# Start-up order of a fused window-attention and Fourier-mixing kernel: bias of image 1, load of the next image, norm of image 2, quarters and eighths

## The chip, the core and the metric

The kernel runs on one core of a Trainium2 chip. A core has a matrix engine (TensorE: PE, with its weight loads as PEld), a vector engine (VectorE: DVE), an activation engine (ScalarE: ACT), GpSimd (POOL), and SyncE (SP), which here only issues DMAs. The metric is the device time of one execution in microseconds (us).

## What is computed

The input `x` has 32 images of 56 x 56 pixels with 128 channels, in fp32. Two layers follow each other, each with a residual. `_gn` is a group norm over an image: 32 groups of 4 channels.

```python
x = x + _L0_conv_ref(_gn(x), ...)   # shifted-window attention
x = x + _L1_conv_ref(_gn(x), ...)   # Fourier mixing, then a feed-forward layer

# layer 0: roll by 3, windows of 7 x 7, 4 heads of 32 channels
qkv  = win @ w_qkv.T
attn = softmax(q @ k.T * scale + rel_bias + mask)
out  = (attn @ v) @ w_proj.T + b_proj              # then roll back

# layer 1: along the width with w0, along the height with w1
y = idct(einsum('bixy,ioy->boxy', dct(x)[..., :32], w))
b = relu((y0 + y1) @ W1 + b1) @ W2 + b2
```

## The kernel before

**The unit of work.** A window row is 7 lines of an image, 8 windows, 392 tokens. An image has 8 window rows. The outer loop counts `cycle`; cycle `r` begins window row `r % 8` of image `r // 8` and carries on older rows and images. A cycle does:

- `attn_qk` for row r: two matmuls on PE, q (L380) and half of k (L389) written by ACT, the other half of k (L397) by DVE. They need `im.w`, the image's scaled weights (`wn`, L364), and `im.bias`.
- `attn_scores` for row r (called in `quarters`): PE L431, then two DVE additions of bias and mask (L439) out of two PSUM banks.
- `attn_max`: a DVE maximum (L449) and a POOL subtraction (L450); `attn_exp` on ACT (L456); `attn_divide`: DVE sum (L461), reciprocal (L463), POOL product (L464).
- `attn_transpose` of earlier rows: PE L475, copies by DVE (L485) and ACT (L483).
- `attn_values` for row r-3 (called in `eighths`): PE L500 into two banks; bank 0 is copied to `oT` by ACT (L533), bank 1 by three DVE instructions (L531).
- `attn_v` for row r (PE L409, copied by ACT L416) and `attn_project` for row r-3: PE with `wproj`, a DVE addition into the image (L548) and a DMA to the scratch tensor `scr`.
- `attn_sums` for row r-4: statistics for layer 1 (DVE L562, ACT L570, DVE L571).

**The Fourier stages.** From cycle 11 on, `fourier(cycle)` names the images in layer 1 and their step c: width transforms at c = 0, height transforms at 1 and 2 (of columns loaded from `scr` into `htok` by `load_columns`), `mix` at 3 to 5 (PE L680, copied by ACT L688), `modes_back` at 5 to 8 (PE L719; ACT L735 or DVE L730 out of PSUM) and feed-forward groups at c in 8, 9, 10, 12 to 15. A cycle is "without feed-forward" if no image in it is at such a c. That holds for every cycle before 19 and, until the last image, for one cycle in eight afterwards.

**PSUM.** There are eight banks, four for attention (`pa`) and four for layer 1 (`pc`). A matmul waits until the last reader of its bank is through.

**Begin of an image.** `image_begin(b)` takes one of two buffers `xl` and loads half of the image; the other half is loaded in the next cycle. `image_groups` transposes it on PE into `xw`, takes statistics, and adds the projection's bias to the image on POOL by `image_bias` (L307, two instructions for two window rows). For image 0 `image_bias` is called in cycles 0 to 3 instead. `image_groups` runs in cycles 4 and 5 for image 1, and in cycle 6 of every eight for the later ones.

**Norm of an image.** `image_norm` is a generator that is driven in four steps, one per `next(norm, None)`: (1) nothing; (2) a chain of twelve small DVE instructions (L334 to L352) and a power on POOL (`rstd`, L356); (3) `nb` on DVE (L361) and `wn` on ACT (L364); (4) a bias by four matmuls and a copy (L368).

**Order.** PE, ACT, DVE and POOL run in exactly the order in which the program calls them: the loop is inside `tc.manual_schedule(engines={ET.PE, ET.Activation, ET.DVE, ET.Pool})`. SP is not in this set. The order of its DMAs is made when the program is built, from the written order and from a model of when their buffers and data are ready.

The calls of a cycle are `first_rows` for cycles 0 to 10. After that they are `halves_first`, (`half_columns`), `eighths`, `quarters`, `full`, `halves_last`. `next_begin` at the end of a cycle starts the load of the next image:

```python
if b + 1 < NB and i == 3:
    images[b + 1] = image_begin(b + 1)
if b + 1 < NB and i == 4 and images[b + 1].half:
    load_part(images[b + 1].x, b + 1, 1)
```

Of the kernel before, what the change touches and what calls it, by code (L numbers as in the profile page):

```python
# [24 lines left out]
NWR = S // WS  # L25
# [23 lines left out]
def swin_fourier_kernel(  # L49
# [20 lines left out]
    nc = tc.nc  # L70
    NB = x.shape[0]
# [195 lines left out]
    def image_groups(im, i):  # L267

        pt = [conv_bank() if i % 4 else attn_bank() for _ in range(2)]
        pts = [
            p[:, : n * S].rearrange("p (j r s) -> p j r s", r=n, s=WS) for p, n in zip(pt, (8, 6))
        ]
        for c in range(7):
            nc.tensor.transpose(  # L276
                pts[c // 4][:, :, 2 * (c % 4) : 2 * (c % 4) + 2],
                im.x[:, WS * i // 2 + c],
                ident_x[:, :, SS:].rearrange("p r (j s) -> p j r s", s=WS),
            )  # L280
        for k in range(2):

            im.xw[i + k] = big.tile([P, RT + JP - WT], F32, tag="xw", name="xw", bufs=10)
            nc.gpsimd.memset(im.xw[i + k][:, RT:], 0.0)
            xw = im.xw[i + k][:, :RT]
            dst = xw.rearrange("p (j r s) -> p j r s", r=WS, s=WS)
            if k:
                nc.scalar.copy(dst[:, :, 0], pts[0][:, :, WS])
                nc.scalar.copy(
                    dst[:, :, 1:].rearrange("p j r s -> p j (r s)"),  # L290
                    pts[1].rearrange("p j r s -> p j (r s)"),
                )
            else:
                nc.scalar.copy(
                    dst.rearrange("p j r s -> p j (r s)"),
                    pts[0][:, :, :WS].rearrange("p j r s -> p j (r s)"),
                )
            nc.vector.bn_stats(im.st[:, i + k], xw)
        if im.b:
            image_bias(im, i)  # L300

    def image_bias(im, i):
# [182 lines left out]
                nc.vector.tensor_copy(aT[:PW, :, :PW], src)  # L485
            im.aT[i].append(aT)

    def attn_values(im, i, r):


        v = v_sb[r % 3]
        po = [attn_bank(), attn_bank()]
        HALF = RT // 2
        po4 = [p[:, :HALF].rearrange("p (r n s) -> p n r s", r=WS, s=WS) for p in po]
        for f in range(2):
            for e in range(2):
                for h in range(NH):
                    for u in range(2):
                        ks = slice(u * JP, u * JP + WT)
                        nc.tensor.matmul(  # L500
                            po4[u][h * HD : (h + 1) * HD, 2 * f + e],
                            lhsT=v[ks, 2 * f + e, h * HD : (h + 1) * HD],
                            rhs=im.aT[i][f][ks, h, e * JP : e * JP + WT],
                            start=True,
                            stop=True,
                        )

        if i % 2 == 0:
            im.oT = work.tile([P, 2 * RT], F32, tag="oT", name="oT")
        oT = im.oT  # L510


        oTr = oT[:, i % 2 * RT : (i % 2 + 1) * RT].rearrange("p (r x) -> p r x", x=S)
        for u in range(2):
            src = po[u][:, :HALF].rearrange("p (r f x) -> p r f x", r=WS, f=2)
            x0 = SS + u * 2 * WS
            if not u:
                dst = bass.AP(
                    oTr.tensor, oTr[:, :, x0:].offset, [oTr.ap[0], [S, WS], [4 * WS, 2], [1, 2 * WS]]
                )  # L520
                parts = [(dst, src)]
            else:
                n = S - 4 * WS - x0
                parts = [
                    (oTr[:, :, x0 : x0 + 2 * WS], src[:, :, 0]),
                    (oTr[:, :, S - n : S], src[:, :, 1, :n]),
                    (oTr[:, :, 0:SS], src[:, :, 1, n:]),
                ]
            for d, f in parts:
                if u:  # L530
                    nc.vector.tensor_scalar(d, f, im.bias[:, 2:3], None, ALU.add)  # L531
                else:
                    nc.scalar.activation(d, f, AF.Identity, bias=im.bias[:, 2:3])  # L533
# [322 lines left out]
    def halves_first(cycle, norm):  # L856
        for im, c in fourier(cycle):
            if c == 0 and cycle > CONV_BEGIN:
                start_stats(im)
        last, j = row(cycle - 4)  # L860
        sums = attn_sums(last, j) if last and cycle > CONV_BEGIN else nothing()
        next(sums)
        im, i = row(cycle)
        if im:
            attn_qk(im, i, False)
        if has_ff(cycle):
            next(norm, None)
        next(sums)
        for im, c in fourier(cycle):
            if c in FF_AT:  # L870
                ff_in(im, FF_AT.index(c))
        for im, c in fourier(cycle):
            if c == 0:
                next(im.stats)
# [38 lines left out]
    def eighths(cycle):  # L913
        im, i = row(cycle - 3)
        if im:
            attn_values(im, i, cycle - 3)

    def full(cycle):

# [19 lines left out]
    def halves_last(cycle, norm):  # L939
        im, i = row(cycle)  # L940
        if im:
            attn_v(im, i, cycle)
        if has_ff(cycle):
            half_columns(cycle)
        half_columns(cycle, True)
        load_back(cycle + 1)
        next_begin(cycle)
        load_first(cycle)
        next(norm, None)
        if row(cycle)[0]:  # L950
            attn_exp(cycle)
            attn_divide(cycle)
        im, j = row(cycle - 3)
        if im:
            last_out(cycle)
            attn_project(im, j)

    def next_begin(cycle):
        b, i = divmod(cycle, NWR)
        if b + 1 < NB and i == 3:  # L960
            images[b + 1] = image_begin(b + 1)
        if b + 1 < NB and i == 4 and images[b + 1].half:
            load_part(images[b + 1].x, b + 1, 1)


# [1 line left out]
    def first_rows(cycle, norm):  # L967
        im, i = row(cycle)
        if im:
            attn_qk(im, i, True)  # L970
        if cycle:
            attn_exp(cycle - 1)
        im3, i3 = row(cycle - 3)
        if im3:
            attn_values(im3, i3, cycle - 3)
        im2, i2 = row(cycle - 2)
        if im2:
            attn_transpose(im2, i2, cycle - 2)
        if cycle:
            attn_divide(cycle - 1)  # L980
        if im:
            attn_scores(im, i, cycle)
            attn_max(cycle)
        if im3:
            attn_project(im3, i3)
        next(norm, None)
        last, j = row(cycle - 4)
        if last:
            for _ in attn_sums(last, j):
                pass  # L990
        if im:
            attn_v(im, i, cycle)
        if cycle < NWR // 2:
            image_bias(im, 2 * cycle)
        if cycle in (4, 5):
            for half in range(2):
                bias_and_mask(nc.gpsimd, 1, cycle - 4, half)
        next_begin(cycle)
        next_groups(cycle)
        if cycle == CONV_BEGIN - 1:  # L1000
            start_stats(im3)
            for _ in attn_sums(im3, i3):
                pass
            attn_exp(cycle)
            attn_divide(cycle)
            last, j = row(cycle - 1)
            attn_transpose(last, j, cycle - 1)

    ET = mybir.EngineType
    with tc.manual_schedule(engines={ET.PE, ET.Activation, ET.DVE, ET.Pool}):  # L1010
# [6 lines left out]
        for cycle in range(NB * NWR + CONV_BEGIN + FF_AT[-1] - NWR + 1):  # L1017
            if cycle < CONV_BEGIN:
                first_rows(cycle, norm)
            else:  # L1020
                halves_first(cycle, norm)
                if not row(cycle - 3)[0]:
                    half_columns(cycle)
                    half_columns(cycle, True)
                    load_first(cycle)
                    last_out(cycle)
                    quarters(cycle)
                    load_back(cycle + 1)
                    continue
                if not has_ff(cycle):  # L1030
                    half_columns(cycle)
                eighths(cycle)
                quarters(cycle)
                if not has_ff(cycle):
                    next(norm, None)
                if row(cycle)[0] and cycle % 2:
                    attn_max(cycle)
                full(cycle)
                halves_last(cycle, norm)
            b, i = divmod(cycle, NWR)  # L1040
            if i == (NWR - 2 if b else NWR - 3) and b + 1 < NB:
                norm = image_norm(images[b + 1])
                next(norm, None)
# [62 lines left out]
```

## Time and profile before

| what | value |
|---|---|
| median of 3 runs | 3616.99 us (3616.63 to 3623.41) |
| profiled execution | 3612.19 us, span 3610.4 us |
| PE busy | 3553.3 us, 98% of the span |
| PEld, DVE, ACT, POOL busy | 78%, 63%, 59%, 38% |
| DMA | 390.30 MB, 16 engines busy 39% to 40% |
| granted TensorE clock, mean | 0.997 |

The profile shows one execution. "Busy" is the time in which an engine works on an instruction; a wait names the engine and line whose instruction ended last before the waiting one began. "L450" is line 450 of the kernel. The window view gives the busy time of each engine within a stretch, and the clock that TensorE was granted there (1.00 is full speed). The timeline lists instructions of one engine in order of time, neighbours of one kind merged. Cycle 4 begins at about 45 us, cycle 7 at 67 us, cycle 8 at 82 us, cycle 12 at 114 us, cycle 15 at 149 us, cycle 16 at 159 us, cycle 17 at 171 us, cycle 18 at 178 us and cycle 19 at 191 us, counted by the first q matmul.

### The profile page before, as it was taken

To read this page: it belongs to the slowest core of one execution; us is meant where nothing else is said; L and a number is where in the kernel's file an instruction comes from. 1 tells how busy PE (TensorE), PEld (TensorE's weight loads), DVE (VectorE), ACT (ScalarE), POOL (GpSimd) and SP (SyncE) were. 2 spreads that over 40 slices of the span, in tenths; PEclk is the share of its full clock that TensorE was granted. 3 is DMA by queue.
4 is the path that set the end of the run, shared out by engine and by line. 5 is a ranking of instruction groups with operands and counts; after the bars stand their busy time and mean duration, and the time that the engine had idled before them with its cause. 6 is when DMAs were issued, how large, how long until landed. Compare 5 with 4: busy or idle time off the path is not lost.

```text
span 3610.4 us, 161666 instructions
## 1 busy us (share of the span) xinstructions
PE 3553.3 (98%) x72192; PEld 2827.3 (78%) x72192; DVE 2256.6 (63%) x4722; ACT 2145.8 (59%) x4044; POOL 1375.3 (38%) x1437
## 2 busy tenths in 40 slices
PE   7899999999999999999999999999999999999999
PEld 5778787777877787877777777878777877777776
DVE  7766666665666666666656666666666666666641
ACT  5555566665666655666556666556665566655553
POOL 6443343433443433434333434343443344343411
PEclk9999999999999999999999999999999999999999
DMA  4334433444434444344444344443444443444343
GB/s 115 95 101 110 118 104 103 109 111 111 111 98 115 109 109 120 98 109 107 114 106 115 95 111 112 112 117 93 112 108 115 107 114 95 114 109 114 95 117 97
DMA packets 687349, 390.30 MB, mean 108 GB/s; under 512 B 39967, under 2 KB 657600, under 8 KB 686400
## 3 DMA queue, kind: packets, MB, share of 16 engines
q1 hardware_dynamic: 686045, 379.65, 39.0%
q8 instruction: 568, 9.31, 1.1%
q14 instruction: 125, 1.02, 0.1%
q10 hardware_dynamic: 611, 0.32, 0.0%
HBM read 218.29 MB, written 161.48 MB: 105 GB/s over the span
## 4 chain that ended last, share of the span: by engine, by line
PE 93%; DVE 4%; ACT 1%; issue 1%; POOL 1%; DMA 0%; SPq 0%; ACTq 0%; POOLq 0%; DVEq 0%
PE pc L112 38%; PE pa L112 15%; PE pa L409 6%; PE pc L680 6%; PE pa L475 6%; PE pc L646 6%; PE pa L431 5%; PE pa L500 4%; PE pc L719 4%; PE pa L276 1%; PE pc L276 1%; DVE a L439 1%; DVE xf L730 0%; DVE oT L531 0%; POOL rstd L617 0%
## 5 line engine op out<-in xcount | busy, mean ns | idle before, releaser
L450 POOL TENSOR_TENSOR a<-a,mx 128x784 f32<-128x784 f32 x256 | 389.8, 1523 | 1390.3 <-DVE mx L449 954.1
L112 PE MATMUL pc<-wff,hid 128*64 128x128 f32 x12544 | 739.9, 273 | 1.5 <-ACT hid L764 1.0
L112 PE MATMUL pc<-xf,wff 128*64 128x512 f32 (+2 forms) x3584 | 718.2, 539 | 1.1 <-DVE xf L730 1.0
L112 PEld LDWEIGHTS pc<-wff,hid 128*64 128x64 f32 x12544 | 702.5, 137 | 7.7 <-ACT hid L764 4.6
L461 DVE TENSOR_REDUCE sm<-a 128x16 f32<-128x784 f32 x256 | 248.3, 970 | 674.2 <-ACT a L456 670.9
L464 POOL TENSOR_TENSOR a<-a,rs 128x784 f32<-128x784 f32 x256 | 389.7, 1522 | 609.1 <-DVE rs L463 553.8
L764 ACT ACTIVATE hid<-pc,b1sb 128x512 f32<-128x512 f32 (+2 forms) x896 | 522.4, 631 | 71.9 <-PE pc L112 68.5
L112 PEld LDWEIGHTS pc<-xf,wff 128*64 128x64 f32 x3584 | 275.7, 137 | 358.9 <-issue 240.3
L380 ACT ACTIVATE q<-pa,bqkv 128x392 f32<-128x392 f32 x256 | 150.5, 588 | 463.1 <-PE pa L112 457.4
L112 PE MATMUL pa<-xw,wn 128*64 128x392 f32 (+1 forms) x2048 | 389.0, 495 | 9.0 <-ACT wn L364 8.3
L531 DVE TENSOR_SCALAR oT<-pa,bqkv 128x98 f32<-128x98 f32 (+2 forms) x768 | 171.1, 278 | 242.5 <-PE pa L500 242.4
L456 ACT ACTIVATE a<-a 128x784 f32<-128x784 f32 x256 | 222.7, 870 | 150.8 <-POOL a L450 148.8
L752 POOL TENSOR_TENSOR res<-res,b2sb 128x512 f32<-128x512 f32 (+2 forms) x256 | 264.6, 1039 | 113.8 <-DMA res<-scr 107.5
L416 ACT COPY v<-pa 128x512 f32<-128x512 f32 x256 | 151.1, 590 | 243.3 <-PE pa L409 243.2
L307 POOL TENSOR_TENSOR xl<-xl,bproj 112x512 f32<-112x512 f32 (+1 forms) x256 | 287.5, 1146 | 0.1
L409 PE MATMUL pa<-wn,xw 128*64 128x128 f32 x4096 | 283.5, 280 | 3.5 <-issue 1.7
L500 PEld LDWEIGHTS pa<-aT,v 49*32 49x32 f32 x16384 | 172.3, 105 | 145.6 <-issue 119.5
L439 DVE TENSOR_TENSOR a<-pa,bm 128x392 f32<-128x392 f32 x512 | 264.9, 560 | 26.5 <-PE pa L431 2.7
L483 ACT COPY aT<-pa 113x452 f32<-113x452 f32 x256 | 139.7, 546 | 208.6 <-PE pa L475 205.3
L475 PE MATMUL pa<-ident,a 113*113 113x113 f32 x2048 | 242.9, 271 | 7.1 <-POOL a L464 3.8
L409 PEld LDWEIGHTS pa<-wn,xw 128*64 128x64 f32 x4096 | 221.3, 137 | 36.0 <-issue 3.2
L449 DVE TENSOR_REDUCE mx<-a 128x16 f32<-128x784 f32 x256 | 246.4, 962 | 4.3
(97 smaller groups left out, 5647.7 us busy)
## 6 DMA issues: line engine op xcount, KB each, us to landing
zscr<-z SPq DMA_DIRECT2D x512, 112.0 KB
htok<-scr SPq DMA_DIRECT2D x256, 196.0 KB
zT<-zscr SPq DMA_DIRECT2D x192, 256.0 KB
res<-scr SPq DMA_DIRECT2D x160, 256.0 KB
out_dram<-res SPq DMA_DIRECT2D x160, 256.0 KB
scr<-xl SPq DMA_DIRECT2D x128, 224.0 KB
xl<-in_x_dram SPq DMA_DIRECT2D x32, 784.0 KB
xl<-in_x_dram SPq DMA_DIRECT2D x32, 672.0 KB
```

What stands on the lines that cost most here:

```text
L112: nc.tensor.matmul(dst[ps], lhsT=lhsT[:, ps], rhs=rhs, start=start, stop=stop)
L307: nc.gpsimd.tensor_tensor(piece, piece, bproj.unsqueeze(1).to_broadcast([TC, e - a, C]), ALU.add)
L409: nc.tensor.matmul(pv[hs, j * C : (j + 1) * C], lhsT=im.xw[i][:, w * WT : w * WT + JP], rhs=im.w[:, 2 * C : 3 * C], start=True, stop=True,)
L439: nc.vector.tensor_tensor(a[:, 2 * hp : 2 * hp + 2, :, 0:WT].rearrange("p u w j -> p w u j"), ps[hp][:, :RT].rearrange("p (w u j) -> p w u ...
L449: nc.vector.tensor_reduce(mx, a3, axis=AX.X, op=ALU.max)
L450: nc.gpsimd.tensor_tensor(a3, a3, mx.unsqueeze(2).to_broadcast([P, 2 * NWR, WT]), ALU.subtract)
L461: nc.vector.tensor_reduce(sm, a3, axis=AX.X, op=ALU.add)
L464: nc.gpsimd.tensor_tensor(a3, a3, rs.unsqueeze(2).to_broadcast([P, 2 * NWR, WT]), ALU.mult)
L475: nc.tensor.transpose(pt[:PW, h * P : h * P + PW], a[:PW, h, 2 * hf : 2 * hf + 2].rearrange("p w j -> p (w j)")[:, :PW], ident[:PW, :PW],)
L500: nc.tensor.matmul(po4[u][h * HD : (h + 1) * HD, 2 * f + e], lhsT=v[ks, 2 * f + e, h * HD : (h + 1) * HD], rhs=im.aT[i][f][ks, h, e * JP : ...
L752: nc.gpsimd.tensor_tensor(res[:m, c0:c1], res[:m, c0:c1], b2sb[:m].unsqueeze(1).to_broadcast([m, c1 - c0, C]), ALU.add,)
L764: nc.scalar.activation(hf[:, :n], ph[:, :n], AF.Relu, bias=b1sb[:, f : f + 1])
```

## The change

1. `image_bias` for image 1 moves out of `image_groups` (cycles 4 and 5) into `first_rows`, one call in each of the cycles 6 to 9.
2. `next_begin` starts the next image at i = 4 instead of 3 and loads its second half at i = 5 instead of 4. `load_first` is called ahead of it.
3. In cycles without feed-forward the step of the norm that stood after `quarters` now stands in `halves_first`, ahead of the scores. This touches steps 2 and 4 of image 2's norm, in cycles 15 and 16. In cycle 15 the three DVE copies of `attn_values` (L531) become ACT instructions.
4. In cycles without feed-forward that have back groups, `quarters` is called ahead of `eighths`. These are cycles 16, 17 and 18.

```diff
-        if im.b:
+        if im.b > 1:
             image_bias(im, i)
...
-    def attn_values(im, i, r):
+    def attn_values(im, i, r, copies):
...
-                if u:
+                if copies[u] is nc.vector:
                     nc.vector.tensor_scalar(d, f, im.bias[:, 2:3], None, ALU.add)
...
-        if has_ff(cycle):
-            next(norm, None)
+        next(norm, None)
         next(sums)
...
-            attn_values(im, i, cycle - 3)
+
+            copies = (nc.scalar, nc.vector)
+            if cycle % NWR == NWR - 1 and not has_ff(cycle):
+                copies = (nc.scalar, nc.scalar)
+            attn_values(im, i, cycle - 3, copies)
...
         load_back(cycle + 1)
+        load_first(cycle)
         next_begin(cycle)
-        load_first(cycle)
         next(norm, None)
...
-        if b + 1 < NB and i == 3:
+        if b + 1 < NB and i == 4:
             images[b + 1] = image_begin(b + 1)
-        if b + 1 < NB and i == 4 and images[b + 1].half:
+        if b + 1 < NB and i == 5 and images[b + 1].half:
             load_part(images[b + 1].x, b + 1, 1)
...
         if cycle < NWR // 2:
             image_bias(im, 2 * cycle)
+        elif cycle >= NWR - 2 and cycle < NWR + 2:
+            image_bias(images[1], 2 * (cycle - NWR + 2))
...
-                eighths(cycle)
-                quarters(cycle)
-                if not has_ff(cycle):
-                    next(norm, None)
+                if has_ff(cycle) or not any(back_groups(c) for _, c in fourier(cycle)):
+                    eighths(cycle)
+                    quarters(cycle)
+                else:
+                    quarters(cycle)
+                    eighths(cycle)
```

## The prediction

> **What bounds the kernel now.** I read the page's busy table first (PE busy 3553.3 us, 98% of the span), then the stages by windows. In this view the columns are: window, its length, busy time of PE, PEld, DVE, ACT, POOL (instructions), granted clock, DMA share, GB/s.
>
> ```profile
> 68.30:71.60 3.30, 1.22 (x68) 0.67 (x64) 3.20 (x5) 1.77 (x3) 3.30 (x6) 1.00 0.46 124
> 71.70:81.80 10.10, 6.95 (x68) 6.18 (x70) 9.69 (x21) 2.74 (x5) 5.55 (x5) 0.50 0.00 0
> 160.50:163.70 3.20, 3.20 (x34) 3.20 (x30) 2.43 (x5) 2.98 (x8) 1.10 (x1) 0.50 0.00 0
> 264.00:3358.00 3094.00, 3083.68 (x63168) 2463.74 (x63166) 1972.58 (x4116) 1870.82 (x3529) 1193.47 (x1232) 1.00 0.40 109
> ```
>
> From 264 us to 3358 us PE lacks 10 us in 3094: nothing of weight can be won there, only lost. The idle time is in the first 200 us, and there the granted clock falls to 0.50 after some gaps. So the next view is PE's waits in that stretch (total us, times, longest):
>
> ```profile
> PE pa L112 <- ACT wn L364: 8.3, 2, 5.1
> PE pa L475 <- POOL a L464: 3.8, 2, 3.4
> PE pa L431 <- ACT k L393: 3.1, 2, 1.7
> PE pa L500 <- issue: 2.2, 1, 2.2
> PE pa L475 <- DVE a L439: 1.8, 1, 1.8
> ```
>
> Two of these the change touches: 3.41 us in cycle 7 (transposes wait for POOL) and 3.26 us at the start of cycle 16 (first matmul of image 2 waits for its scaled weights, wn). The timeline shows what precedes the first, POOL's and DVE's own queues (start, duration, engine, line):
>
> ```profile
> 69.17 2.23 POOL L307 TENSOR_TENSOR xl<-xl,bproj 112x512 f32<-112x512 f32 x2
> 71.34 1.53 POOL L464 TENSOR_TENSOR a<-a,rs 128x784 f32<-128x784 f32 x1
> 72.82 1.52 POOL L450 TENSOR_TENSOR a<-a,mx 128x784 f32<-128x784 f32 x1
> ```
> ```profile
> 69.44 3.47 DVE L325 TENSOR_SCALAR gmeans<-gsums 128x32 f32<-128x32 f32 x1
> 72.94 1.45 DVE L340 TENSOR_TENSOR turned<-turned,gmeans 128x32 f32<-128x32 f32 x1
> 74.42 0.19 DVE L341 TENSOR_TENSOR turned<-turned 128x32 f32<-128x32 f32 x1
> 76.50 0.66 DVE L531 TENSOR_SCALAR oT<-pa,bqkv 128x98 f32<-128x98 f32 x3
> ```
>
> L464's input was ready at 66.1 (reciprocal L463, 65.84 + 0.25); it starts 5.2 us later, behind image 1's bias (L307). Two tiny DVE steps of the norm, 0.18 and 0.19 us elsewhere, last 3.47 and 1.45 us while POOL works, and hold L531, for which PE's scores wait. One pair of steady rows shows the same in every later image, where the norm runs beside POOL:
>
> ```profile
> 807.15 0.56 DVE L325 TENSOR_SCALAR gmeans<-gsums 128x32 f32<-128x32 f32 x1
> 807.75 1.45 DVE L340 TENSOR_TENSOR turned<-turned,gmeans 128x32 f32<-128x32 f32 x1
> 810.31 0.15 DVE L352 SCALAR_TENSOR_TENSOR ve<-back 128x1 f32<-128x1 f32 x1
> ```
>
> **Bias of image 1 (cycles 4, 5 to 6-9).** POOL loses four calls of 2.24 us, 9.0 us, ahead of L464 of row 5. L464 then runs at 66.2-67.7 and L450 of row 6 (mx ready 68.06) at 68.2-69.7. On DVE, L325 is let in at about 69.75 in place of 72.91, L340 takes 0.19, the rest of the chain 1.26 (75.66 - 74.39), so it ends near 71.3 in place of 75.66; two reductions (0.55 each) and L531 follow, to 73.0. PE transposes at 69.6 and can do the last 28 scores at 73.1 where it did them at 77.3: 4.2 us. In that cycle the scores, projection and v took 1.57 + 1.47 + 1.67 = 4.7 us at clock 0.50; the same steps two cycles earlier took 0.89 + 0.80 + 0.87 = 2.6. PE's idle time there falls from 5.3 us to about 1.75, so I take the clock as full: 2.1 more. Against it: nb (L361) still waits for POOL's L450 (1.29 us before, likewise after) and DVE, nearly full in cycle 8, is late for its copies: 0.6 back. Term: -5.7; ends -6.3 and -3.0 (clock halved again and DVE later). The moved bias, 2.24 us in each of cycles 6 to 9, lies in POOL's idle time, which is 2.8, 4.7, 3.6 and 2.9 us ahead of the next L464; without that cover each call would cost up to 2.24.
>
> [...]
>
> **Norm of image 2 ahead of scores (cycles 15, 16), its copies on ACT.** In cycle 15 the chain starts at 153.1 in place of 155.18. But POOL is busy to 155.84 with L307 and L464, as in the steady rows above, where the chain takes 4.2 us (806.29 to 810.46) in place of 2.5 (155.18 to 157.72). So ve comes 0.45 us earlier, and wn with it: the 3.26 us gap shrinks to 2.8. The chain now stands ahead of L571, the scores' two L439 (1.03) and the maximum L449, which ends 1.2 us later; behind L449 are POOL's L450, ACT's exp, the q and k copies and z copies of cycle 16. The three oT copies go to ACT, which idles 1.36 us before L416: nothing. In cycle 16 PE's four bias matmuls only change place.
>
> [...]
>
> **Quarters ahead of eighths (cycles 16, 17, 18; no others lack feed-forward and have back groups).** The second back group needs the banks of the two z copies. They end at 164.64; now near 165.8. Scores (0.8), values (0.75), transposes (1.78) follow: cycle 16's v starts at 169.9 in place of 169.28, +0.6. In cycle 17 the values (0.74) used to run while PE waited for k (L397); now they come after the scores, and L531 (0.66) stands between L439 and L449. Scores wait for L397 till 176.3 (175.39 before), and cycle 18 starts at 179.6 in place of 177.85. In cycle 18 DVE's L730 (2.2) no longer follows L531, which gives 0.35 back: +1.4 at cycle 19. PE's gaps of 1.7 to 2.9 us in these cycles may halve the clock as at 160.5; I add 0.6 (a 3.4 us window loses at most 1.7, mostly behind other waits). Term of cycles 15 to 18: +2.0; ends -3.3 (the gap of cycle 16 goes and nothing comes back) and +4.5.
>
> **Image load a cycle later.** SP's order is not the written one:
>
> ```profile
> 59.37 0.38 SPq L745 DMA_DIRECT2D res<-scr  x1
> 109.73 4.55 SPq L118 DMA_DIRECT2D xl<-in_x_dram  x5
> ```
>
> A load of cycle 19 (190 us) is issued at 59 us, and both halves of image 2 go together though written a cycle apart: SP takes what has its buffer. The buffer is free once the width transforms of cycle 3 of the 8 have read it, before and after alike. So I expect the same issue times: 0. The htok loads are ahead of it already (860.4 against 867.5 in one image), and the reordering of `load_first` does nothing. If the load does move, image 2's leaves cycle 12, where PE's 2.19 us "issue" gap fell in the same stretch as that load and cost 2.6 us more at half clock: -4.8. It is needed in cycle 6 of the 8, some 14 us after SP would then issue it, so a move alone starves no one.
>
> **Sum.** -5.7 + 2.0 + 0 = -3.7 us. The profiled execution was 3612.19 us (span 3610.4, 1.8 around it), 4.8 below the median of 3616.99; the difference goes onto the median: 3613.3. Less than 0.2% (7.2 us) is about what a measurement of this kernel cannot tell from no change.
>
> **Rivals.** *More than expected (0.22).* The load leaves cycle 12 (-4.8), with the other terms as above: 3608.5. For it: the gap lies where the load's traffic saturated the DMA. Against it: SP's issue order just shown.
> *The gain does not arrive (0.14).* DVE and the half clock hold cycle 7 to -3.0 and cycles 15 to 18 give +3 back: 3617. For it: DVE is busy 9.69 of 10.10 us in the window of cycle 7. Against it: most of that is blocked time.
> *Slower (0.11).* The load does move a cycle and meets PE's instruction stream in a dense stretch of every image, as it may have in cycle 12: 2.19 us in each of 30 images is +66, 3679; a fifth of the images gives 3626. It decides from 0.36 us an image ((7.2 + 3.7)/30). Against it: in the new place, the end of the next cycle, the same kinds of step follow.
>
> **How the numbers follow.** The forecast, within 0.2%, has 0.53: its own range is 3609 to 3618. Faster by over 0.2%: 0.20 of the first rival and 0.04 of the forecast's tail, 0.24. Slower: 0.09 of the last and 0.01 of the second, 0.10. The rest, 0.66, is the same. The range 3606.5 to 3620 leaves out about 0.08 below and 0.11 above.
>
> **What would show it.** Right: L464 of row 5 starts by 66.5 us, L325 in cycle 6 under 1 us, cycle 8 starts 5 to 6 us earlier; the wait for wn in cycle 16 is still over 2 us; L325/L340 in cycle 15 last 0.5 and 1.4 us; xl is still issued right after the width transforms; later images take 110.1 us as now (first q matmul to first q matmul, eight cycles on). Wrong: xl a cycle later, no "issue" gap in cycle 12, a wait for wn under 1 us, or other than 110.1 us an image.

## The result and the profile after

The changed kernel took 3617.97 us (median of 4 runs, 3614.64 to 3620.66) and the kernel before 3619.18 us (4 runs, 3616.63 to 3623.41): a ratio of 0.9995, interval 0.9978 to 1.0012, no difference that this measurement can tell. (The prediction's 3616.99 us is the median of the first three of these four runs; the fourth took 3621.37.) In a longer comparison (e13_after_again below) the ratio was 0.9991, interval 0.9982 to 1.0000. The forecast had been 3613.3 us in a range of 3606.5 to 3620.

The windows of after's profile that answer to those of before come first: cycle 7, then the gap of cycle 16, then the later images (columns as before: window, length, busy PE, PEld, DVE, ACT, POOL, granted clock, DMA share, GB/s).

```profile
71.20:74.60 3.40, 2.36 (x77) 1.74 (x76) 3.02 (x14) 3.11 (x7) 1.79 (x3) 1.00 0.29 71
74.60:81.40 6.80, 6.14 (x62) 5.07 (x64) 6.66 (x13) 1.43 (x4) 5.85 (x5) 0.51 0.10 26
...
153.10:156.50 3.40, 1.08 (x8) 0.48 (x8) 3.19 (x9) 0.61 (x1) 0.55 (x1) 1.00 0.63 189
156.60:160.00 3.40, 3.40 (x36) 3.18 (x34) 0.87 (x3) 1.64 (x5) 1.52 (x1) 0.50 0.02 5
...
264.00:3358.00 3094.00, 3080.59 (x63062) 2459.66 (x63060) 1969.27 (x4106) 1868.73 (x3524) 1189.01 (x1229) 1.00 0.41 109
```

In the first of these windows PE idles 1.04 us of 3.40 (its gaps in cycle 7 add up to 1.6 us, before to 5.3), and still the clock is halved for the 6.8 us that follow. After 264 us PE lacks 13 us in 3094 where it lacked 10.

PE's waits in the first 200 us of after (total us, times, longest):

```profile
PE pa L112 <- ACT wn L364: 7.8, 2, 5.1
PE pa L431 <- DVE k L397: 5.8, 3, 2.4
...
PE pa L500 <- issue: 1.6, 1, 1.6
...
PE pa L475 <- POOL a L464: 0.4, 1, 0.4
```

The wait for POOL's L464 has gone from 3.8 to 0.4 us. The wait for k (L397) is now 5.8 us in three places; before it was 2.3, 1.70 in cycle 14 and 0.58 in cycle 17. Now 1.69 of it is in cycle 17 and 2.43 in cycle 18. These two come with the quarters; what they cost is taken up with the prediction's term below.

The stages, each from the first q matmul of one cycle to that of another, in us, worked out from the profiled execution of each kernel. "Half" is the time between 60 and 200 us in which the granted clock was 0.50.

| kernel | 4-8 | 8-12 | 12-15 | 15-20 | 24-248 | half |
|---|---|---|---|---|---|---|
| before | 37.1 | 32.3 | 35.0 | 59.8 | 3094.3 | 20.5 |
| after | 32.9 | 33.2 | 33.2 | 62.4 | 3100.6 | 20.5 |
| e13_after_again | 32.7 | 33.2 | 33.5 | 62.4 | 3095.4 | 20.5 |
| e1_bias | 32.0 | 32.7 | 36.6 | 60.1 | 3096.8 | 20.5 |
| e12_bias_again | 30.5 | 33.7 | 34.1 | 59.7 | 3097.8 | 6.8 |
| e2_load | 37.0 | 32.7 | 34.7 | 60.2 | 3096.3 | 17.1 |
| e3_norm | 36.5 | 32.3 | 34.9 | 59.9 | 3099.9 | 13.7 |
| e4_quarters | 36.8 | 32.7 | 34.7 | 62.3 | 3100.1 | 23.9 |
| e5_bias_both_norm | 32.7 | 32.4 | 35.0 | 60.2 | 3098.1 | 10.2 |
| e9_without_bias | 37.0 | 32.7 | 32.6 | 62.5 | 3098.3 | 20.5 |
| e10_load_forced | 37.5 | 32.8 | 33.2 | 60.7 | 3100.7 | 20.5 |
| e11_old_quarters | 32.3 | 32.9 | 34.1 | 60.2 | 3099.4 | 10.2 |
| e14_bias_and_one_load | 30.6 | 33.4 | 31.2 | 60.1 | 3094.5 | 6.8 |

Two columns tell the edits apart in every kernel. Cycles 4 to 8 take 36.5 to 37.5 us with the old place of the bias and 30.5 to 32.9 with the new one. Cycles 15 to 20 take 62.3 to 62.5 us with quarters ahead of eighths and 59.7 to 60.7 without. Within these bounds the columns still move with the halved clock. Cycles 12 to 15 follow the clock even more: cycle 14 takes 16.5 us in the eight profiles in which the clock was halved there and 15.0 in the five others (before, after, e13, e9 and e14). The last column of times varies by 6 us without any order in it: the changed kernel itself gave 3100.6 and 3095.4. That, with 2.2 us more ahead of cycle 4 (46.9 for 44.7 us; e13 44.8), and not the change, is why after's profiled execution (3618.27 us, span 3616.5) is above that of before (3612.19). In every kernel the quickest of the later images took 110.1 us and the middle one 110.2 to 110.6.

### The profile page after: what moved, and what is told of

The parts are those of the page before. It is cut to its first block, busy times and chain, and to the rows that moved or that the text cites. A ratio compares the mean times of both kernels' runs of the same rounds, so it can differ in the third digit from the quotient of the medians.

```text
span 3616.5 us, 161667 instructions
## 1 busy us (share of the span) xinstructions
PE 3559.0 (98%) x72192; PEld 2832.2 (78%) x72192; DVE 2252.7 (62%) x4719; ACT 2147.2 (59%) x4047; POOL 1374.1 (38%) x1437
## 4 chain that ended last, share of the span: by engine, by line
PE 91%; DVE 5%; ACT 1%; POOL 1%; issue 1%; DMA 0%; SPq 0%; POOLq 0%; DVEq 0%; ACTq 0%
PE pc L112 37%; PE pa L112 14%; PE pa L409 6%; PE pc L680 6%; PE pa L475 6%; PE pc L646 6%; PE pa L431 5%; PE pa L500 4%; PE pc L719 4%; PE pa L276 1%; PE pc L276 1%; DVE a L439 1%; DVE xf L730 1%; POOL a L450 1%; ACT a L456 0%
## 5 line engine op out<-in xcount | busy, mean ns | idle before, releaser
L450 POOL TENSOR_TENSOR a<-a,mx 128x784 f32<-128x784 f32 x256 | 389.3, 1521 | 1391.8 <-DVE mx L449 927.2
L464 POOL TENSOR_TENSOR a<-a,rs 128x784 f32<-128x784 f32 x256 | 389.2, 1520 | 611.8 <-DVE rs L463 537.7
L764 ACT ACTIVATE hid<-pc,b1sb 128x512 f32<-128x512 f32 (+2 forms) x896 | 523.0, 631 | 73.7 <-PE pc L112 70.1
L380 ACT ACTIVATE q<-pa,bqkv 128x392 f32<-128x392 f32 x256 | 150.4, 587 | 465.0 <-PE pa L112 459.3
L531 DVE TENSOR_SCALAR oT<-pa,bqkv 128x98 f32<-128x98 f32 x765 | 170.6, 278 | 246.2 <-PE pa L500 246.2
L307 POOL TENSOR_TENSOR xl<-xl,bproj 112x512 f32<-112x512 f32 (+1 forms) x256 | 287.2, 1145 | 0.0
L431 PE MATMUL pa<-k,q 64*64 64x98 f32 x8192 | 236.8, 250 | 13.1 <-DVE k L397 5.8
## 6 DMA issues: line engine op xcount, KB each, us to landing
zscr<-z SPq DMA_DIRECT2D x512, 112.0 KB
```

The costliest lines, as they stand in the source:

```text
L307: nc.gpsimd.tensor_tensor(piece, piece, bproj.unsqueeze(1).to_broadcast([TC, e - a, C]), ALU.add)
L431: nc.tensor.matmul(ps[hp][HALVES[e], pr * 2 * WT : (pr + 1) * 2 * WT], lhsT=q[cs, w * WT : w * WT + JP], rhs=k_sb[cs, :, w], start=True, s ...
L450: nc.gpsimd.tensor_tensor(a3, a3, mx.unsqueeze(2).to_broadcast([P, 2 * NWR, WT]), ALU.subtract)
L464: nc.gpsimd.tensor_tensor(a3, a3, rs.unsqueeze(2).to_broadcast([P, 2 * NWR, WT]), ALU.mult)
L764: nc.scalar.activation(hf[:, :n], ph[:, :n], AF.Relu, bias=b1sb[:, f : f + 1])
```

## The experiments

The first four kernels each have one part of the change alone. They ran on one chip beside the kernel before (3618.6 us, median of 31 runs).

**The bias of image 1 alone.**

```diff
-        if im.b:
+        if im.b > 1:
...
+        elif cycle >= NWR - 2 and cycle < NWR + 2:
+            image_bias(images[1], 2 * (cycle - NWR + 2))
```

> Only the bias of image 1 is moved (cycles 4, 5 to 6-9). Stage times are from first q matmul to first q matmul; before: cycles 4 to 8 take 37.1 us, 15 to 20 take 59.8; with the whole change 32.9 and 62.4. Theory (the bias gives the gain, the norm and the quarters give part of it back): 4 to 8 takes 31 to 33, 15 to 20 takes 59 to 61, and the kernel is 4 to 6 us faster than before. Rival (the loss in cycles 15 to 20 comes with the gain, because the same waits are only reached earlier): 4 to 8 takes 31 to 33 and 15 to 20 about 62.5, 1 to 2 us faster than before in all.

Measured: 3613.27 us, ratio 0.9985, interval 0.9975 to 0.9994. Cycles 4 to 8 are 5.2 us shorter than before. In this profile too the clock is halved (0.52 in the window from 74.1 us on) after the remaining gaps of cycle 7:

```profile
70.70:74.10 3.40, 1.80 (x36) 1.38 (x36) 3.22 (x12) 2.57 (x5) 2.34 (x3) 1.00 0.12 31
74.10:77.50 3.40, 3.40 (x33) 3.22 (x32) 3.26 (x7) 0.10 (x1) 2.44 (x3) 0.52 0.00 0
```

So the bias alone makes the kernel faster, by about as much as its term said (5.7 us).

**The image load alone.**

```diff
-        next_begin(cycle)
         load_first(cycle)
+        next_begin(cycle)
...
-        if b + 1 < NB and i == 3:
+        if b + 1 < NB and i == 4:
...
-        if b + 1 < NB and i == 4 and images[b + 1].half:
+        if b + 1 < NB and i == 5 and images[b + 1].half:
```

> Only the load of the next image is written a cycle later and load_first ahead of it. Theory (the order of SP's DMAs is made from when buffers are free, so nothing moves): image 2's five load DMAs go out together after the width transforms of cycle 11, near 110 us, later images take 110.1 us and a few tenths, cycle 12 to 13 takes 11.5 to 13.4 us with an issue gap of 1.6 to 2.2 us on PE, and the time is that of before within the noise. What differs from before is then the noise of one program: where the half-clock windows fall and how often later images lose some tenths. Rival (the load moves): image 2's load goes out after 125 us, the issue gap of cycle 12 is gone, cycle 12 to 13 takes under 10 us, and the kernel is about 5 us faster.

Measured: 3618.16 us, ratio 1.0000, interval 0.9990 to 1.0009. Every engine has the same instructions as before, and SP's DMAs stand in the same order: written a cycle later, the loads are issued at the same place (4.1 us after the first `htok` loads: 111.90 for 107.81 us, in before 109.73 for 105.64). This kernel is therefore a second profile of the kernel before. Its wait for issue in cycle 12 is 2.1 us (2.2 before), but the clock is halved from 73.7, 141.9 and 162.4 us on where in the first it was from 71.6, 119.4 and 160.4. Where the clock halves belongs to the run, not only to the program.

**The norm of image 2 ahead of the scores, alone** (with the copies of cycle 15 on ACT).

```diff
-        if has_ff(cycle):
-            next(norm, None)
+        next(norm, None)
...
+            if cycle % NWR == NWR - 1 and not has_ff(cycle):
+                copies = (nc.scalar, nc.scalar)
...
-                if not has_ff(cycle):
-                    next(norm, None)
```

> Only part 3: the norm of image 2 ahead of the scores in cycles 15 and 16, with the three copies of cycle 15 on ACT. Theory (the chain is held by POOL's bias of image 2 and now stands ahead of scores and maximum): DVE's L340 in cycle 15 lasts 1.4 us, PE's wait for wn at cycle 16 is 2.6 to 2.8 us (3.26 before), the maximum L449 of row 15 comes about 1.2 us later against its cycle's start, and 15 to 20 takes 59.5 to 61 us (59.8 before). Rival (the norm ahead is worth the gap): wait for wn under 1 us, 15 to 20 takes 57 us or less. 4 to 8 takes 37 us in both.

Measured: 3620.01 us, ratio 1.0005, interval 0.9996 to 1.0015. The hold of 1.4 us that was expected of L340 did not come. POOL was further ahead of DVE here than in after: L464 had ended at 154.89 us, 0.07 us before L340 began, where in after L340 began 0.13 us after the start of L464. The chain was hardly held up (DVE, start, duration):

```profile
154.42 0.51 DVE L325 TENSOR_SCALAR gmeans<-gsums 128x32 f32<-128x32 f32 x1
154.96 0.19 DVE L340 TENSOR_TENSOR turned<-turned,gmeans 128x32 f32<-128x32 f32 x1
```

PE's waits between 156 and 180 us then are:

```profile
PE pa L112 <- ACT wn L364: 1.5, 1, 1.5
PE pa L500 <- ACT q L380: 1.4, 2, 1.0
PE pa L500 <- DVE xl L548: 0.8, 1, 0.8
```

The wait for wn fell from 3.3 to 1.5 us, but PE met two others a few instructions on, together 1.8 us after 1.0 and 0.8: q, which ACT wrote late behind its exp, and the DVE addition L548 behind the scores' additions. Cycle 15 to 16 is 1.8 us shorter (8.08 for 9.86), cycle 16 to 17 is 1.75 longer (13.78 for 12.03); each kernel has one halved stretch of 3.4 us in these two cycles. Moving the norm was worth nothing here, even where it freed the chain.

**Quarters ahead of eighths, alone.**

```diff
-                eighths(cycle)
-                quarters(cycle)
+                if has_ff(cycle) or not any(back_groups(c) for _, c in fourier(cycle)):
+                    eighths(cycle)
+                    quarters(cycle)
+                else:
+                    quarters(cycle)
+                    eighths(cycle)
```

> Only part 4: quarters ahead of eighths in cycles 16, 17 and 18. Theory (values used to fill PE's wait for k, and L531 now stands between the additions L439 and the maximum L449): PE waits 1 us or more for k (L397) ahead of the scores of cycle 17, 0.6 before, and 15 to 20 takes 61 to 62 us (59.8 before). Rival (scores a step earlier bring the softmax chain earlier): 15 to 20 takes 59 us or less. The wait for wn is 3.2 us and 4 to 8 takes 37 us in both.

Measured: 3620.15 us, ratio 1.0004, interval 0.9995 to 1.0014; cycles 15 to 20 take 62.3 us, 2.1 to 2.4 more than in the three kernels above. Of its waits between 150 and 200 us the second is the new one, 2.7 us for k in place of 0.6; the 2.1 us for q (L380) and the 0.9 us for L571 of before are not among them:

```profile
PE pa L112 <- ACT wn L364: 3.3, 1, 3.3
PE pa L431 <- DVE k L397: 2.7, 2, 1.6
```

PE does not idle longer for it: 8.1 us between the starts of cycles 15 and 20, for 9.8 in e2. It is the clock that differs, halved for 13.7 us there and for 3.4 in e2. What the order costs in time is clear in the stage; in the total it is below what these runs can tell.

The next four kernels combine parts. They ran beside the kernel before at 3616.91 us (31 runs).

**Bias of image 1, norm ahead, and the bias of image 2 moved too.** The kernel is e3_norm with the bias of image 1 in cycles 6 to 9, as in e1, and that of image 2 in cycles 15 to 18, so that POOL is free beside the chain of cycle 15.

```diff
-        if im.b:
+        if im.b > 2:
...
+        if 2 * NWR - 1 <= cycle < 2 * NWR + 3:
+            image_bias(images[2], 2 * (cycle - 2 * NWR + 1))
```

> The bias of image 1 is moved as in the change, that of image 2 from cycle 14 to cycles 15-18 (one call behind each division), and the norm of image 2 stands ahead of the scores with its three copies on ACT; the quarters stay behind the eighths, the load is as before. So POOL is free beside the norm's chain. Theory (the chain is held by POOL's bias; without it the chain is short, but cycle 16 is then held by ACT's exp and q copies, so little arrives): L325 and L340 in cycle 15 last 0.2 us each, the wait for wn is 1.0 to 1.6 us, and cycles 15 to 20 take 58.5 to 60 us; 4 to 8 takes 32, the kernel 3 to 6 us less than before. Rival (POOL's hold on the chain was all that kept the norm from paying): 15 to 20 takes 57 us or less and the kernel is 7 us or more faster than before.

Measured: 3613.15 us, ratio 0.9990, interval 0.9981 to 1.0000. L325 and L340 take 0.18 and 0.19 us with the bias of image 2 gone from beside them; in after, with POOL at work on L307 and L464, they take 0.45 and 1.45. PE's gap for wn is 1.14 us, and again 1.0 and 0.8 us for q and L548 follow; cycles 15 to 20 take 60.2 us. The norm ahead of the scores was worth nothing here even without that work of POOL beside it.

**The whole change without the bias part.**

```diff
-        if im.b > 1:
+        if im.b:
...
-        elif cycle >= NWR - 2 and cycle < NWR + 2:
-            image_bias(images[1], 2 * (cycle - NWR + 2))
```

> The whole change but for its first part: the bias of image 1 stays in cycles 4 and 5. Theory (parts 3 and 4 cost 2 to 3 us by themselves): 4 to 8 takes 37 us, 15 to 20 takes 61.5 to 63 (59.8 before), PE waits 1.6 us for k in cycle 17 and 2.4 in cycle 18, and the kernel is 1 to 4 us slower than before. Rival (they cost only because the bias brings the rows forward): 15 to 20 takes 60 or less and the time is that of before or under it.

Measured: 3620.70 us, ratio 1.0010, interval 1.0001 to 1.0019: slower by 3.8 us. With the 5.3 us that the bias gained from e1_bias this gives -1.5 us for the whole; measured were -1.2 and, below, -3.0.

**The load of every image really moved.** A POOL memset of one column, placed where the load is written, makes SP's DMAs wait for it. The load itself is that of e2_load.

```diff
+        if b > 1:
+            nc.gpsimd.memset(t[:, k * h : (k + 1) * h, 0:1], 0.0)
         for a, e, p, src in chunks_of(x, b, k * h, (k + 1) * h):
             nc.sync.dma_start(t[p, a:e], src)
```

> The load is written a cycle later as in the change, and made to move: a small POOL memset ahead of each half (from image 2 on) touches the tile, so the DMA can't go earlier than the place where it is written. Theory (the burst of the load beside the transforms of cycle 12 delays what PE waits for there): image 2's first half goes out after 118 us, the issue gap of 1.6 to 2.4 us in cycle 12 is gone, cycle 12 to 13 takes 8.5 to 9.5 us, later images stay at 110.1 us and a few tenths, and the kernel is 2 to 5 us faster than before. Rival 1 (the gap is PE's own instruction stream, whatever the load does): the gap stays. Rival 2 (the moved burst meets a dense stretch in every image): later images take 110.5 us or more at their least and the kernel is over 7 us slower.

Measured: 3619.78 us, ratio 1.0009, interval 0.9999 to 1.0019. SP issues image 2's halves at 126.6 and 135.5 us, and the wait for issue in cycle 12 is gone. Cycles 12 to 15 take 33.2 us (before 35.0, e2_load 34.7), cycles 15 to 20 then 60.7 (59.8, 60.2). The whole kernel was not faster, as was expected (2 to 5 us), but 2.9 us slower in the median, with an interval that still holds 1. From cycle 24 to 248 it took 3100.7 us, where the kernels that leave the load alone took 3094.3 to 3100.6. No dense stretch has gone wrong by 2 us an image; a loss of a tenth or two in each image would not show against this spread.

**The whole change with eighths ahead of quarters again.**

```diff
-                if has_ff(cycle) or not any(back_groups(c) for _, c in fourier(cycle)):
...
+                eighths(cycle)
+                quarters(cycle)
```

> The whole change but for its last part: eighths stay ahead of quarters in cycles 16 to 18. Theory (the new order of the quarters is what costs): 15 to 20 takes 59.5 to 61 us in place of 62.4, the wait for k in cycle 17 is back at 0.6 us, and the kernel is 4 to 6 us faster than before, as with the bias alone. Rival (the norm's place costs as much as the quarters): 15 to 20 takes 61 to 62 us and the kernel is 2 to 4 us faster than before.

Measured: 3614.24 us, ratio 0.9992, interval 0.9982 to 1.0001; cycles 15 to 20 take 60.2 us. The 2.3 us more that the whole change spends there are those of the quarters. The total gained 2.7 us, less than the 4 to 6 expected, and its interval just reaches 1. As in e3, L340 took 0.19 us and PE waited 1.5 us for wn.

The last three ran together, beside the kernel before at 3613.75 us (27 runs).

**The bias alone again, and the whole change again** (the edits as above).

> The bias of image 1 moved, nothing else, measured again beside the whole change. If the bias part is the only part with an effect for the better (e1_bias): about 5 us below the kernel before, ratio 0.9985 (0.9978 to 0.9992), and cycles 4 to 8 between 31.5 and 33 us. If its 5 us were a matter of one run: ratio 0.9995 or more.

> The whole change again. If quarters ahead of eighths costs 2 to 2.5 us in cycles 16 to 19 and the norm and the load are worth nothing: 2 to 3 us above the bias alone of this call, ratio to the kernel before 0.9990 to 0.9998, cycles 15 to 20 between 62 and 63 us. If the stages only shift noise: the same time as the bias alone, within 1 us.

Measured: bias alone 3608.98 us, ratio 0.9988 (0.9979 to 0.9996); whole change 3610.72 us, ratio 0.9991 (0.9982 to 1.0000). The whole change lies 1.7 us above its bias part, the direction and nearly the size expected, but the intervals overlap. In the profile of the bias alone the clock was not halved in cycle 7:

```profile
70.10:73.50 3.40, 2.86 (x81) 1.82 (x78) 3.02 (x14) 3.19 (x7) 1.69 (x2) 1.00 0.28 71
73.50:76.90 3.40, 2.25 (x54) 1.96 (x54) 3.30 (x10) 1.34 (x3) 2.82 (x4) 1.00 0.01 2
```

The waits of cycle 7 are the same as in after (1.15 and 1.16 us for L531), and cycles 4 to 8 take 30.5 us instead of 32.9. PE idles 2.2 us in both; it is busy 28.3 us instead of 30.7, so the 2.4 us between them are the halved clock.

**The bias, and the load of image 2 alone held back.** The kernel is e12_bias_again with the edits of e2_load and e10_load_forced, but the memset only for image 2 (`if b == 2`).

> The bias of image 1, and the load of image 2 alone really held back (a GpSimd memset of a column of each half of its buffer stands ahead of its DMAs, in cycles 12 and 13; later images keep their loads where they were). If the load is what made TensorE wait in cycle 12: no wait over 1 us for issue there, cycles 12 and 13 shorter by 1.5 to 4 us, nothing changed after 264 us, 3610 to 3612 us, 1.5 to 3 below the bias alone. If that time is given back in cycles 13 to 20 as in e10_load_forced: cycles 12 to 20 as in the bias alone within 1 us, and the same total.

Measured: 3607.03 us (3604.44 to 3608.89, 11 runs), ratio 0.9982, interval 0.9973 to 0.9990, the quickest of all. PE's waits between 100 and 150 us, first of the bias alone, then of this kernel (its line numbers are two higher):

```profile
PE pa L431 <- DVE k L397: 2.6, 2, 1.7
PE pa L409 <- ACT oT L533: 1.6, 2, 1.3
PE pa L500 <- issue: 1.6, 1, 1.6
```

```profile
PE pa L433 <- DVE k L399: 2.9, 3, 1.7
PE pa L411 <- ACT oT L535: 1.6, 2, 1.3
...
PE pa L411 <- issue: 0.2, 1, 0.2
```

The wait for issue has left, and cycles 12 to 20 take 91.3 us (31.2 + 60.1) against 93.8. Not all of these 2.5 us are the load's. Cycle 12 gives 1.4 (8.7 for 10.0), at full clock in both. Cycle 14 gives 1.5, because the clock was halved there in e12 and not here, and cycles 15 to 20 give 0.4 back. The median is 1.95 us below the bias alone; the intervals of the two overlap, so the gain of the load is shown in cycle 12 and only likely in the total.

## Why the prediction was right, step by step

**The bias.** The prediction's walk through cycle 6 can be laid beside e13_after_again, in which cycle 4 began within 0.1 us of before. POOL, then DVE:

```profile
66.38 1.52 POOL L464 TENSOR_TENSOR a<-a,rs 128x784 f32<-128x784 f32 x1 [1.42 <-DVE rs L463]
68.28 1.52 POOL L450 TENSOR_TENSOR a<-a,mx 128x784 f32<-128x784 f32 x1 [0.38 <-DVE mx L449]
...
71.94 2.23 POOL L307 TENSOR_TENSOR xl<-xl,bproj 112x512 f32<-112x512 f32 x2
74.75 1.52 POOL L464 TENSOR_TENSOR a<-a,rs 128x784 f32<-128x784 f32 x1 [0.58 <-DVE rs L463]
```

```profile
69.58 0.26 DVE L325 TENSOR_SCALAR gmeans<-gsums 128x32 f32<-128x32 f32 x1
69.87 0.19 DVE L340 TENSOR_TENSOR turned<-turned,gmeans 128x32 f32<-128x32 f32 x1
...
71.18 0.15 DVE L352 SCALAR_TENSOR_TENSOR ve<-back 128x1 f32<-128x1 f32 x1
...
72.17 0.66 DVE L531 TENSOR_SCALAR oT<-pa,bqkv 128x98 f32<-128x98 f32 x3
```

L464 stands at 66.4 (forecast 66.2), L450 at 68.3 (68.2), L340 takes 0.19, the chain ends at 71.3 (71.3), L531 at 72.8 (73.0). The moved L307 lies in POOL's idle time: L464 starts 0.58 us after L307 has ended. PE's idle time in cycle 7 was to fall from 5.3 us to about 1.75; it is 1.7 in all seven kernels with the new place. The step that failed is the clock, "so I take the clock as full: 2.1 more". It held in two of the seven kernels with the new place (e12, e14: cycles 4 to 8 shorter by 6.6 us) and not in after, e13, e1, e5 and e11, which kept 6.8 or 3.4 us of half clock and gained 4.2 to 5.2. The sign "cycle 8 starts 5 to 6 us earlier" did not come in the changed kernel: counted from cycle 4, it starts 4.2 and 4.4 us earlier in its two profiles. Cycles 8 to 12 gave back up to 1.4 us where 0.6 was forecast. The term was -5.7 with ends of -6.3 and -3.0; cycles 4 to 12 gave -3.4 in after, -4.9 in e1 and -5.2 in e12.

**The norm of image 2.** Forecast was that POOL's L464 holds the chain up, so that wn gains only 0.45 us and the gap shrinks to 2.8. In after's DVE timeline:

```profile
150.88 0.45 DVE L325 TENSOR_SCALAR gmeans<-gsums 128x32 f32<-128x32 f32 x1
151.37 1.45 DVE L340 TENSOR_TENSOR turned<-turned,gmeans 128x32 f32<-128x32 f32 x1
...
153.94 0.15 DVE L352 SCALAR_TENSOR_TENSOR ve<-back 128x1 f32<-128x1 f32 x1
```

The two steps last 0.45 and 1.45 us (forecast 0.5 and 1.4) and the gap of cycle 16 is 2.7. L340 ends at 152.8, as POOL's L464 does (151.24 + 1.53). In before it ended at 74.39, and POOL's L450 at 74.34. The 3.47 us of L325 before lie beside three POOL instructions, since the row of L307 merges two and L464 follows: L325 ended at 72.91 and L464 at 72.87.

That POOL holds the chain is not a property of the change alone. The prediction read it off a profile with a full clock in cycle 14, and it came in the three kernels with the norm ahead in which cycle 14 ran at full clock (after, e13, e9: L340 1.45 us, wait for wn 2.7). In e3 and e11 the clock was halved in cycle 14; POOL then had L464 behind it before L340 came, which took 0.19 us, and the wait for wn was 1.5. The end of the range that the prediction kept for this term, -3.3 with "the gap of cycle 16 goes and nothing comes back", did not come about: e3, e11 and e5 free the chain and the time comes back within one cycle.

**The quarters.** Forecast were PE gaps of 1.7 to 2.9 us in cycles 16 to 18 and k as the new wait; measured in after are 1.69 and 2.43 us for k (L397) in cycles 17 and 18, besides 2.7 for wn:

```profile
172.85 0.91 PE L431 MATMUL pa<-k,q 64*64 64x98 f32 x32 [1.69 <-DVE k L397]
...
181.86 0.91 PE L431 MATMUL pa<-k,q 64*64 64x98 f32 x32 [2.43 <-DVE k L397]
```

Cycles 15 to 20 grew by 2.7 us where +2.0 was forecast; e4 and e11 put 2.0 to 2.4 of it on the quarters. The direction and nearly the size came as forecast, but not by the forecast path, which was 1.4 us of later starts behind the new waits and 0.6 for the clock. These are cycles 15 to 20 of before, of after and of e11, the whole change without the new order (columns as above):

```profile
149.19:208.94 59.75, 50.44 (x1197) 40.52 (x1194) 40.97 (x94) 32.25 (x60) 23.41 (x24) 0.97 0.35 98
146.14:208.57 62.43, 52.74 (x1196) 42.65 (x1194) 42.11 (x91) 33.11 (x63) 23.38 (x24) 0.92 0.33 94
146.32:206.48 60.16, 50.47 (x1196) 40.35 (x1194) 40.69 (x91) 32.65 (x63) 21.95 (x21) 0.97 0.35 97
```

PE idles 9.3, 9.7 and 9.7 us. The waits for k have taken the place of others (in before 2.1 us for q). What has grown is PE's busy time, by 2.3 us for the same work. In after the clock is halved for 10.2 us here and in the two others for 3.4; in all four kernels with the new order it is halved for 6.8 us in cycle 18, behind the second wait for k. So the term that was mis-sized is the 0.6 us for the clock, an estimate of the author's that no run shows, and the sum of the two came out near by luck. Whether the waits would have cost time at full clock stays open, since no profile has the new order without that halved stretch.

**The load.** SP issues it as before:

```profile
108.51 4.84 SPq L118 DMA_DIRECT2D xl<-in_x_dram  x5
...
869.00 1.12 SPq L118 DMA_DIRECT2D xl<-in_x_dram  x2
...
874.70 2.30 SPq L118 DMA_DIRECT2D xl<-in_x_dram  x3
```

Term 0, as forecast. The first rival, in which the load leaves cycle 12, names an effect that e10 and e14 show and that this change does not set off: they move the load, and the wait for issue in cycle 12 (2.2 us in before) goes. Its price of 4.8 us holds only where the clock is halved behind the gap. Cycle 12 took 13.4 us in before, 8.7 and 9.1 with the load moved (e14, e10), and 10.0 to 10.8 in the seven kernels that have the load there and a full clock. So the load is worth about 1 to 2 us in cycle 12, and 4.3 to 4.7 against the profile that the prediction read. The last rival, a moved load that hits a dense stretch, is excluded by e10 at the prices that it was given (13 us and more); a smaller loss in the later images is not.

**The sum.** -3.7 us was forecast, -1.2 and -3.0 were measured. The sum was right because no term missed by more than 2.3 us, and because part of the misses cancelled by luck. In after the bias gave 2.3 us less than forecast and cycles 15 to 20 cost 0.7 more, but cycles 12 to 15, for which there was no term, took 1.8 us less (33.2 for 35.0), above all because the clock was halved for 3.4 us in cycle 12 and not for 6.8. And 3613.3 itself is 4.7 us from the first median, which is less than the 5.4 us by which the median of the kernel before moved between the comparisons (3613.75 to 3619.18).

## What to carry over

A stall that an engine causes by work nobody waits for yet was worth removing here (5.3 us in e1_bias), and it can be priced by walking the queues of two engines forward; a step moved ahead to serve one waiter only pays if the next waits (here q and L548, 1.0 and 0.8 us in e3_norm) are also early. Before crediting an edit of a DMA's place, compare where the DMA was issued: in e2_load the load was written a cycle later and still went out 4.1 us after the `htok` loads, as before. Where the clock was halved after some gaps in one run and not in another (in cycle 7 in after, not in e12), price every term with and without the halved stretch, and look at idle and busy time apart before blaming a wait for a lost microsecond.

## What was not expected of the chip

**The clock was halved after stretches in which PE was still busy, and not after every such one.** Between 60 and 200 us the halved stretches of before last 10.2, 6.8 and 3.4 us (from 71.6, 119.4 and 160.4 us on), those of after 6.8, 3.4, 3.4 and 6.8 us (from 74.7, 119.1, 156.6 and 183.9 us on). In the 3.40 us ahead of the first of them PE was busy for 1.32 us in before and for 2.36 us in after; ahead of the others it was 1.77 and 1.35 us in before and 1.80, 1.08 and 1.64 us in after. Such a share alone did not always bring it: in after PE was busy for 1.71 of 3.40 us from 170.2 us on, and the next 3.40 us ran at full clock. In cycle 7 the same waits of 1.15 and 1.16 us for L531 were followed by 6.8 us of half clock in after and by none in e12, where PE was busy for 2.25 of 3.40 us from 73.5 us on. What decides is not shown.

**PE stopped beside the burst of a load.** With image 2's five load DMAs issued from 105.3 to 112.0 us on, PE stopped for 1.6 to 2.4 us for "issue" in cycle 12, in each of the eleven profiles that have the load there. With the load at 121.6 us or later (e10, e14) it did not. The DMA records of the traces show what was late. Blocks of 16 KB come on an instruction queue (q8), 568 of them in before. That they are PE's is an estimate from their number: 72192 matmuls and 72192 weight loads make 254 to a block, and the engine with the next most instructions, DVE, has 4722. In before a block came from 117.20 to 118.41 us, 8.3 us after the start of the one before it, and PE went on at 119.97; in after one came from 115.33 to 116.60 us, 7.6 us after the one before it, and PE went on at 118.16, in both 1.6 us after the block had ended. In before no block moved from 110.4 to 117.1 us, while the load and `htok` filled the 16 DMA engines; in e14 one did from 108.1 to 112.5 us, with the engines almost free (queue, packets, MB, share of 16 engines):

```profile
q1 hardware_dynamic: 3163, 1.59, 101.2%
```

```profile
q8 instruction: 1, 0.02, 1.4%
q1 hardware_dynamic: 19, 0.01, 1.0%
```

From these times the author's estimate is that PE waited for its own instructions; no record shows what a block held, nor why it started late while the other queue was full.
